# A transformer block with routed experts on one core: attention's DRAM exchange as one store and one load, and sequence 15 in it too

## The chip, the cores and the metric

One core of a Trainium2 chip runs the whole program. The metric is the device time of one execution in microseconds (us). Before the change it is 1090.54 us, the median of three runs (1088.64 to 1091.8).

## What is computed

Sixteen sequences of 256 tokens with 256 features pass through one block: a layer norm with a shift per sequence, attention with 16 heads of 64 features whose queries and keys are normalised per head, a residual, and then eight experts, each of which takes the 512 tokens of all 4096 with the highest gate. Everything is float32.

```python
h = _ln(x, ln1_g, ln1_b) + shift
qkv = (h @ Wqkv.T).reshape(b, n, 3, H, HD)
q = _ln(qkv[:, :, 0].transpose(0, 2, 1, 3), qn_g, qn_b)
k = _ln(qkv[:, :, 1].transpose(0, 2, 1, 3), kn_g, kn_b)
attn = softmax(einsum('bhnd,bhmd->bhnm', q, k) / sqrt(HD))
o = einsum('bhnm,bhmd->bhnd', attn, v)
x = x + o.transpose(0, 2, 1, 3).reshape(b, n, H * HD) @ Wout.T
gate = softmax(tok @ Wgate.T)
vals, idx = top_k(gate.T, bs // E)
y = gelu(ln(tok[idx]) @ fc1s.T + b1s) @ fc2s.T + b2s
tok = tok.at[idx].add(y * vals)
```

## The kernel before, in words

**Groups and quads.** For each sequence, `First` normalises and turns the tokens (`hT`). `Group(b, g, t)` multiplies 128 tokens by 512 columns of `wq`: g 0 and 1 are queries, 2 and 3 keys, 4 and 5 values. The mean over each head's 64 features is taken out of the weights beforehand (`center`, L600 to L607, once for each of 8 pieces), so that only the sum of squares is left to do: `square` on ACT, `stats` (L705) on DVE, `power` on POOL, `scale` (L721) on DVE. `Quad(b, d)` does four heads in two steps i of two heads j: `scores` (L813) on PE into four PSUM buffers `sc`, `maxima` (L821) on DVE, `exps` (L830) on ACT with the row sums, `invert` (L837), `normalise` (L841) on POOL, `product` (L900) on PE, `evict` (L915) on ACT. `Tail` projects, adds the residual, stores tokens and norms and computes the gates.

**Two ways to turn a tile.** Queries, keys and probabilities must change places between partitions and columns. Sequences 0 and 15 (`DIRECT`) do it on PE: `transposes` (L730, L881), then an ACT copy out of PSUM (L742, L888). The other fourteen use an exchange. DVE turns 32x32 blocks (L754, L851) into a tile `kb` or `pb`; `away` stores it (512 KB) to a DRAM tile whose rows hold four pieces of 1 KB and one of padding (L761, L859); `back` loads it with four DMAs of 128 KB, each to 32 partitions 32q to 32q+31 (L773, L873). Queries and keys then get gain and bias on ACT in `affine` (L781, L789). All these DMAs are issued by SP, in one queue.

**The order.** Every step is entered in a `Plan` with its engine, an assumed duration, what it needs and makes. `PLACES` holds one number for each step, found offline; the steps are issued in the order of these numbers, so each engine has a fixed order. Sorted by them, the first routing (`Routing.turn` L1028, then 30 rounds of `compare_less` L1091, `count_over` L1100 and `decide` L1115) follows the gates of sequence 14, with the later quads and the tail of sequence 15 between its rounds, and dummy matmuls (`fill`, L551) where PE has nothing else. The lists, the gather and the 16 expert jobs come after it.

The scores read the keys of an exchanged sequence piece by piece, so that their columns come in the order (k t m) in which `turn` cuts them:

```python
keys = plain(kTs[self.b]) if direct else (
    kTs[self.b].rearrange("p g k t h m -> p g h (k t) m")
)
```

Of the kernel before, what the change touches and what calls it, by code (L numbers as in the profile page):

```python
# [9 lines left out]
F32 = mybir.dt.float32  # L10
# [8 lines left out]
P = 128  # L19
# [15 lines left out]
SQ = 32  # L35
# [29 lines left out]
def kernel(  # L65
# [83 lines left out]
    def make_others():  # L149
# [21 lines left out]
    DIRECT = (0, B - 1)  # L171
# [11 lines left out]
        0.3, 0, 3.3, 4.02, 3.75, 5.04, 4.42, 7.26, 0, 0, 8, 9.39, 21.59, 15.62, 11.2, 13.11,  # L183
        17.01, 18.4, 0, 0, 0, 0, 0, 0, 0, 3.5, 4.21, 5.54, 4.52, 5.23, 6.09, 6.6, 7.26, 10.88,
        12.83, 15.02, 15.97, 19.79, 26.15, 26.82, 14.6, 16.55, 20.39, 21.18, 23.31, 28.69, 29.8,
        16.33, 18.28, 20.99, 23.06, 25.36, 27.79, 28.46, 20.58, 22.53, 23.91, 24.94, 27, 28.24,
        29.13, 24.1, 26.05, 33.83, 36.09, 29.35, 31.3, 32.01, 32.8, 34.94, 36.73, 37.55, 31.08,
        33.03, 33.74, 34.68, 36.66, 53.28, 54.22, 37.45, 40.14, 40.85, 42.51, 44.49, 48.92, 51.33,
        39.18, 41.13, 41.84, 44.39, 46.57, 52.83, 53.55, 47.04, 49.88, 49.37, 52, 32.81, 35.54,
        36.58, 38.73, 40.91, 41.63, 34.34, 35.13, 39.64, 41.35, 42.12, 38.46, 43.11, 35.71, 37.26,  # L190
        38.22, 40.69, 41.79, 42.61, 37.86, 39.18, 41.6, 42.67, 44.05, 40.42, 46.02, 47.26, 44.13,
        45.37, 46.16, 50.43, 53.73, 55.38, 45.97, 48.92, 51.34, 54.17, 54.89, 50.16, 57, 45.15,
        47.17, 47.96, 53.16, 63.68, 68.13, 47.77, 50.37, 52.25, 64.12, 67.64, 51.61, 70.34, 71.58,
        55.11, 56.95, 58.1, 60.54, 66.44, 67.15, 56.35, 57.14, 59.63, 78.31, 81.13, 59.36, 83.25,
        56.13, 59.53, 64.4, 68.49, 77.87, 78.83, 58.15, 59.06, 67.58, 80.48, 81.62, 66.42, 84.27,
        86.99, 74.97, 76.5, 77.37, 83.28, 91.94, 92.75, 77.1, 79.32, 82.37, 90.48, 91.2, 80.91,
        94.7, 81.36, 83.07, 83.86, 89.48, 96.74, 97.55, 85.48, 87.48, 90.39, 94.26, 96.51, 89.21,
        101.81, 103.78, 115.15, 119.13, 120.28, 120.28, 121.51, 122.02, 123.82, 124.54, 127.81,
        128.58, 118.62, 122.45, 124.6, 123.6, 124.46, 125.96, 131.29, 132, 134.85, 135.67, 0,
        14.5, 15.21, 24.51, 12.59, 13.3, 22.98, 42.23, 43.1, 51.1, 53.05, 53.76, 54.55, 57.55,  # L200
        58.75, 60.22, 62.17, 62.88, 63.82, 65.82, 66.61, 58.34, 60.44, 61.15, 61.94, 63.92, 65.21,
        66.01, 67.37, 70.57, 72.17, 76.37, 61.95, 63.9, 64.61, 65.7, 67.68, 68.47, 69.27, 70.63,
        73.83, 75.43, 80.28, 64.71, 66.66, 68.61, 70.56, 66.88, 68.83, 69.54, 70.33, 72.31, 73.1,
        71.36, 73.46, 74.17, 74.96, 77.7, 78.49, 73.24, 75.19, 75.9, 76.84, 79.1, 80.3, 81.1,
        82.46, 85.66, 87.26, 91.69, 75.99, 78.33, 79.7, 80.49, 82.47, 83.67, 84.47, 85.83, 89.03,
        90.63, 95.66, 78.75, 82.11, 85.14, 88.44, 82.38, 84.88, 86.03, 87.54, 88.6, 84.28, 85.07,
        88.45, 89.51, 87.27, 90.63, 92.63, 95.83, 97.43, 106.44, 90.92, 92.16, 93.24, 96.03,
        97.14, 92.76, 94.2, 96.94, 98.95, 95.76, 99.75, 101.11, 104.31, 105.91, 111.23, 114.89,
        95.72, 97.75, 98.54, 105.78, 106.84, 98.35, 104.27, 106.69, 108.65, 105.51, 109.45,
        111.11, 114.31, 116.23, 129.4, 100.79, 102.03, 102.82, 107.6, 111.66, 102.63, 105.23,  # L210
        108.51, 112.87, 106.47, 113.67, 115.03, 118.46, 120.66, 130.42, 131.51, 107.46, 109.86,
        111.01, 118.96, 120.13, 109.26, 110.05, 114.35, 118.52, 114.08, 125.1, 127.2, 130.51,
        133.3, 141.66, 108.48, 111.06, 112.93, 115.26, 116.69, 110.46, 111.97, 116.17, 117.3,
        114.85, 118.1, 119.46, 123, 125.2, 140.64, 142.75, 112.25, 115.02, 115.88, 121.61, 127.2,
        114.25, 117.33, 122.52, 129.35, 121.34, 130.15, 132.1, 135.7, 138.5, 144.42, 124.04,
        125.39, 126.18, 128.68, 131.68, 125.99, 127.14, 129.59, 132.81, 128.41, 133.61, 135.3,
        138.5, 140.5, 145.44, 148.04, 162.09, 166.05, 167.29, 167.2, 168.45, 170.6, 176.27,
        177.75, 178.81, 179.57, 165.56, 169.54, 171.6, 170.69, 171.55, 172.1, 179.26, 182.41,
        182.94, 184.62, 0, 25.96, 26.82, 28.77, 24.84, 27.58, 28.44, 80.92, 82.6, 87.02, 88.97,
        90.12, 91.3, 93.36, 94.15, 88.75, 90.7, 91.41, 93.18, 95.16, 96.53, 92.53, 95.16, 95.93,  # L220
        97.85, 99.83, 101.03, 101.83, 103.19, 106.39, 109.11, 113.89, 97.33, 99.5, 100.43, 101.22,
        103.23, 104.02, 105.91, 107.91, 111.11, 112.71, 118.29, 99.06, 106.19, 109.35, 116.84,
        102.83, 107.18, 108.05, 109.42, 112.27, 117.91, 104.71, 106.68, 107.45, 111.3, 113.48,
# [1414 lines left out]
```

## Time and profile before

| | before |
|---|---|
| median of three runs | 1090.54 us |
| the profiled execution | 1091.3 us |
| its span, first to last instruction | 1089.5 us |
| granted PE clock, mean | 0.993 |
| PE busy | 1050.4 us |
| POOL busy | 617.5 us |
| DMA: SP's and ACT's queue (q1), share of 16 engines | 69.9% |
| DMA packets under 2 KB | 139440 of 167700 |

PE is the tensor engine and PEld its weight loads, which overlap with matmuls; DVE, ACT and POOL are the vector, scalar and GpSimd engines, SP the one that issues DMAs. A row of a group names the line of the code, the engine, the operation, output and input tiles, shapes and the count, then busy time in all, the mean of one, and the idle time ahead of it with what ended it. Busy times are unions: two overlapping matmuls count once.

### The profile page before, as it was taken

To read this page: it belongs to the slowest core of one execution; us is meant where nothing else is said; L and a number is where in the kernel's file an instruction comes from. 1 tells how busy PE (TensorE), PEld (TensorE's weight loads), DVE (VectorE), ACT (ScalarE), POOL (GpSimd) and SP (SyncE) were. 2 spreads that over 40 slices of the span, in tenths; PEclk is the share of its full clock that TensorE was granted. 3 is DMA by queue.
4 is the path that set the end of the run, shared out by engine and by line. 5 is a ranking of instruction groups with operands and counts; after the bars stand their busy time and mean duration, and the time that the engine had idled before them with its cause. 6 is when DMAs were issued, how large, how long until landed. Compare 5 with 4: busy or idle time off the path is not lost. (4 is left out here: it accounts for less than half of the span.)

```text
span 1089.5 us, 18716 instructions
## 1 busy us (share of the span) xinstructions
PE 1050.4 (96%) x5611; PEld 686.6 (63%) x5611; DVE 809.4 (74%) x2257; ACT 592.3 (54%) x1656; POOL 617.5 (57%) x997
## 2 busy tenths in 40 slices
PE   6999999999999999999999999999988999999996
PEld 4555646555454655555565555656667888888885
DVE  6658888889788797898888887885678588655440
ACT  1768666666566665675666656675612322332331
POOL 3676776778667686667757666665501333333332
PEclk9999999999999999999999999999999999999998
DMA  6025899999999999998999999985130556655661
GB/s 214 1 78 165 269 276 304 291 281 257 283 292 280 280 299 290 289 280 263 277 299 286 265 302 265 321 260 164 61 102 20 149 161 199 186 171 163 192 203 20
DMA packets 167700, 238.56 MB, mean 219 GB/s; under 512 B 17328, under 2 KB 139440, under 8 KB 167600
## 3 DMA queue, kind: packets, MB, share of 16 engines
q1 hardware_dynamic: 159680, 227.08, 69.9%
q0 software_dynamic: 6144, 8.39, 4.2%
q10 hardware_dynamic: 1776, 1.90, 0.5%
q8 instruction: 45, 0.74, 0.3%
q14 instruction: 55, 0.45, 0.1%
HBM read 136.64 MB, written 100.66 MB: 218 GB/s over the span
## 5 line engine op out<-in xcount | busy, mean ns | idle before, releaser
L688 PE MATMUL pm<-wq,hT 128*128 128x512 f32 x768 | 362.1, 607 | 10.1 <-DVE qk L721 3.9
L841 POOL TENSOR_SCALAR pr<-pr,sums 128x256 f32<-128x256 f32 x512 | 237.6, 485 | 102.6 <-DVE sums L837 95.0
L830 ACT ACTIVATE pr<-sc,nmax 128x256 f32<-128x256 f32 x512 | 237.7, 482 | 92.3 <-DVE nmax L821 75.2
L688 PEld LDWEIGHTS pm<-wq,hT 128*128 128x128 f32 x768 | 137.1, 191 | 165.3 <-issue 131.3
L103 POOL TENSOR_TENSOR ss<-ss,neghalf 128x8 f32<-128x8 f32 x128 | 211.2, 1650 | 10.7
L821 DVE TENSOR_REDUCE nmax<-sc 128x2 f32<-128x512 f32 x256 | 165.3, 672 | 19.4 <-PE sc L813 19.1
L851 DVE STREAM_TRANSPOSE pb<-pr 128x512 f32<-128x512 f32 x224 | 150.0, 689 | 15.9 <-POOL pr L841 9.4
L813 PE MATMUL sc<-kT,qT 64*128 64x256 f32 x1024 | 136.8, 396 | 1.0 <-ACT kT L789 0.6
L701 ACT ACTIVATE sq<-pm 128x512 f32<-128x512 f32 x128 | 76.4, 605 | 102.5 <-PE pm L688 100.5
L900 PE MATMUL po<-prT,v 128*64 128x256 f32 x1024 | 129.0, 387 | 1.3 <-DMA prT<-blocks 1.3
L813 PEld LDWEIGHTS sc<-kT,qT 64*128 64x128 f32 x1024 | 91.3, 186 | 50.3 <-issue 28.9
L1319 POOL DMA_INDIRECT out<-y,idx x32 | 51.3, 1604 | 120.6 <-DVE y L1313 66.0
L1286 PE MATMUL ph<-xT,w 128*128 128x256 f32 x512 | 117.8, 383 | 0.0
L1302 PE MATMUL py<-w,hid 128*128 128x256 f32 x512 | 116.3, 380 | 0.0
L926 PE MATMUL pw<-wo,oT 128*128 128x256 f32 x512 | 115.3, 382 | 0.0
L926 PEld LDWEIGHTS pw<-wo,oT 128*128 128x128 f32 x512 | 96.2, 190 | 20.9 <-issue 6.0
L830 ACT ACTIVATION_READ_ACCUMULATOR pr<-sc,nmax 128x1 f32 x512 | 109.2, 213 | 0.0
L900 PEld LDWEIGHTS po<-prT,v 128*64 128x64 f32 x1024 | 66.5, 136 | 66.0 <-issue 20.1
L705 DVE TENSOR_REDUCE ss<-sq 128x8 f32<-128x512 f32 x128 | 85.0, 669 | 28.8 <-ACT sq L701 28.3
L1293 ACT ACTIVATE hid<-ph,vec 128x256 f32<-128x256 f32 x128 | 60.4, 474 | 84.4 <-PE ph L1286 79.4
L1302 PEld LDWEIGHTS py<-w,hid 128*128 128x128 f32 x512 | 95.6, 190 | 12.8
L1286 PEld LDWEIGHTS ph<-xT,w 128*128 128x128 f32 x512 | 95.4, 190 | 12.8
(141 smaller groups left out, 1098.3 us busy)
## 6 DMA issues: line engine op xcount, KB each, us to landing
blocks<-pb SPq DMA_DIRECT2D x112, 512.0 KB, 4.7
prT<-blocks SPq DMA_DIRECT2D x448, 128.0 KB, 4.1
kblocks<-kb SPq DMA_DIRECT2D x56, 512.0 KB, 4.1
w<-in_fc2T SPq DMA_DIRECT2D x16, 1024.0 KB, 5.8
w<-in_fc1T SPq DMA_DIRECT2D x16, 1024.0 KB, 8.3
qraw<-kblocks SPq DMA_DIRECT2D x112, 128.0 KB, 4.0
kT<-kblocks SPq DMA_DIRECT2D x112, 128.0 KB, 4.1
out<-tok SPq DMA_DIRECT2D x32, 128.0 KB, 3.9
```

The source lines that it names most:

```text
L103: nc.gpsimd.tensor_tensor(dst, src, neghalf[:, : src.shape[1]], ALU.pow)
L688: nc.tensor.matmul(self.pm, hTs[self.b][:, c, bass.ts(self.t, P)], wq[:, c, bass.ts(self.g, GW)], start=(c == 0), stop=(c == DC - 1),)
L705: nc.vector.tensor_reduce(self.ss[:, 0, :], self.sq.rearrange("p (h d) -> p h d", d=HD), AX.X, ALU.add,)
L813: nc.tensor.matmul(self.sc[i, j][:, t, :], qTs[self.b][rows, hp, bass.ts(t, P)], keys[rows, hp] if direct else keys[rows, hp // 4, hp % 4] ...
L821: nc.vector.tensor_reduce(self.nmax[i, j], self.sc[i, j], AX.X, ALU.max, negate=True)
L830: nc.scalar.activation(self.pr[i, j][:, t, :], self.sc[i, j][:, t, :], AF.Exp, bias=self.nmax[i, j][:, t : t + 1], scale=1.0, accum_out=se ...
L841: nc.gpsimd.tensor_scalar(self.pr[i, j][:, t, :], self.pr[i, j][:, t, :], self.sums[i][:, 1, j, t : t + 1], 1.0, ALU.mult, ALU.mult,)
L851: nc.vector.transpose(self.pb[i][:, :, :, j].rearrange("p k c t n -> p t k c n"), self.pr[i, j].rearrange("p t (k c m) -> p t k c m", c=TB ...
L900: nc.tensor.matmul(self.po[j * HD : (j + 1) * HD, i, :], vs[self.b][:, c, bass.ts(4 * self.d + 2 * i + j, HD)], prT[:, j, c] if self.b in ...
L926: nc.tensor.matmul(self.pw, oTs[self.b][:, hp // 2, self.t, hp % 2, :], wo[:, hp, :], start=(hp == 0), stop=(hp == HP - 1),)
L1286: nc.tensor.matmul(self.ph[f], self.w1[:, c, bass.ts(f, P)], self.xT[:, c, :], start=(c == 0), stop=(c == DC - 1),)
L1302: nc.tensor.matmul(self.py[i], self.hid[:, f, bass.ts(i, P)], self.w2[:, f, :], start=(f == 0), stop=(f == FC - 1),)
```

## The change

The exchange gets another map. A 128-wide piece goes to partitions 4m+q, q being one of four column pieces, instead of 32q+m. In DRAM the tile has no padding, and the partition order (m q) is then one run of it for each of the four blocks, so that `back` is one DMA of 512 KB to all 128 partitions. To make this the right order:

- the host puts the query and key columns of `Wqkv` in an order of (q, head, feature/4) within each group of 512, so `center`, `stats` and `scale` sum and scale over four pieces of 16 for each head; `center` takes three operations instead of two;
- for sequence 0, which still transposes its queries and keys on PE, `scale` writes them back in natural order, with a step of four words;
- the scores read the keys in natural token order (t k m), and `exps` of exchanged quads read PSUM with a step of four words, so that `pr` is written in the order (q c m).

Only sequence 0 is `DIRECT` now. `OFFS` are the quads that still turn their probabilities on PE: all four of sequence 0 and the quads 2 and 3 of sequence 15. Sequence 15's queries, keys and quads 0 and 1 (its first 8 heads) use the exchange. `PLACES` is new throughout: 3883 numbers for 3883 steps instead of 3863.

```diff
@@ -168,7 +168,7 @@
-    DIRECT = (0, B - 1)
+    DIRECT, OFFS = (0,), {(b, d) for b in (0, B - 1) for d in range(HP // 2)} - {(B - 1, 0), (B - 1, 1)}
...
@@ -180,349 +180,352 @@
     PLACES = (
...
@@ -599,12 +602,14 @@
         def center(g, c):
-            w3 = wq[:, c, bass.ts(g, GW)].rearrange("p (h d) -> p h d", d=HD)
+            w3 = wq[:, c, bass.ts(g, GW)].rearrange("p (q e d) -> p q e d", q=QB, e=8)
             ws = stat.tile([P, 8], F32, tag="ws", bufs=2, name="ws")
-            nc.vector.tensor_reduce(ws, w3, AX.X, ALU.add)
-            nc.vector.scalar_tensor_tensor(
-                w3, ws.unsqueeze(2).to_broadcast([P, 8, HD]), -1.0 / HD, w3, ALU.mult, ALU.add
-            )
+            nc.vector.tensor_reduce(ws, w3.rearrange("p q e d -> p e q d"), AX.XY, ALU.add)
+            nc.vector.tensor_scalar_mul(ws, ws, -1.0 / HD)
+            nc.vector.tensor_tensor(w3, w3, by_head(ws), ALU.add)
+
+        def by_head(x):
+            return x.unsqueeze(1).unsqueeze(3).to_broadcast([P, QB, 8, HD // QB])
         class Norm:
@@ -703,8 +708,8 @@
             def stats(self):
                 self.ss = stat.tile([P, 2, 8], F32, tag="ss", name="ss")
                 nc.vector.tensor_reduce(
-                    self.ss[:, 0, :], self.sq.rearrange("p (h d) -> p h d", d=HD),
-                    AX.X, ALU.add,
+                    self.ss[:, 0, :], self.sq.rearrange("p (q e d) -> p e q d", q=QB, e=8),
+                    AX.XY, ALU.add,
                 )
             def power(self):
@@ -718,10 +723,13 @@
                 if src is None:
                     self.qk = work.tile([P, GW], F32, tag="qk", bufs=3, name="qk")
                     engine, src = nc.vector, self.pm
+                if self.b in DIRECT:
+                    dst = self.qk.rearrange("p (e d q) -> p q e d", q=QB, e=8)
+                else:
+                    dst = self.qk.rearrange("p (q e d) -> p q e d", q=QB, e=8)
                 engine.tensor_tensor(
-                    self.qk.rearrange("p (h d) -> p h d", d=HD),
-                    src.rearrange("p (h d) -> p h d", d=HD),
-                    self.ss[:, 1, :].unsqueeze(2).to_broadcast([P, 8, HD]), ALU.mult,
+                    dst, src.rearrange("p (q e d) -> p q e d", q=QB, e=8),
+                    by_head(self.ss[:, 1, :]), ALU.mult,
                 )
             def transposes(self):
@@ -753,13 +761,13 @@
                     kb.append(work.tile([P, QB, TB, HP // 2, SQ], F32, tag="pb", bufs=3, name="kb"))
                 nc.vector.transpose(
                     kb[0][:, :, self.t],
-                    self.qk.rearrange("p (h q d) -> p q h d", q=QB, d=SQ),
+                    self.qk.rearrange("p (q h d) -> p q h d", q=QB, d=SQ),
                 )
             def away(self, kb):
-                self.blocks = dram.tile([QB, SQ, QB + 1, N], F32, tag="blocks", bufs=4, name="kblocks")
+                self.blocks = dram.tile([QB, SQ, QB, N], F32, tag="blocks", bufs=4, name="kblocks")
                 nc.sync.dma_start(
-                    self.blocks[:, :, :QB].rearrange("k d q n -> (k d) (q n)"),
+                    self.blocks.rearrange("k d q n -> (k d) (q n)"),
                     kb[0].rearrange("p q t h m -> p (q t h m)"),
                 )
@@ -769,10 +777,7 @@
                 else:
                     self.raw = self.keys()[:, self.g - 2]
                 raw = self.raw.rearrange("p k t h m -> p k (t h m)")
-                for q in range(QB):
-                    nc.sync.dma_start(
-                        raw[bass.ts(q, SQ)], self.blocks[:, :, q].rearrange("k d n -> d k n")
-                    )
+                nc.sync.dma_start(raw, self.blocks.rearrange("k d q n -> (d q) k n"))
             def affine(self):
                 if self.g < 2:
@@ -801,10 +806,11 @@
             def scores(self, i):
                 hp = 2 * self.d + i
-                direct = self.b in DIRECT
-                keys = plain(kTs[self.b]) if direct else (
-                    kTs[self.b].rearrange("p g k t h m -> p g h (k t) m")
-                )
+                whole = self.b in DIRECT
+                if whole:
+                    keys = plain(kTs[self.b])
+                else:
+                    keys = kTs[self.b].rearrange("p g k t h m -> p g h t k m")
                 for j in range(2):
                     self.sc[i, j] = ps.tile([P, TB, N], F32, tag="sc", bufs=4, name="sc")
                 for t in range(TB):
@@ -812,7 +818,7 @@
                         rows = slice(j * HD, (j + 1) * HD)
                         nc.tensor.matmul(
                             self.sc[i, j][:, t, :], qTs[self.b][rows, hp, bass.ts(t, P)],
-                            keys[rows, hp] if direct else keys[rows, hp // 4, hp % 4],
+                            keys[rows, hp] if whole else keys[rows, hp // 4, hp % 4],
                             start=True, stop=True,
                         )
@@ -827,8 +833,12 @@
                     self.sums[i] = stat.tile([P, 2, 2, TB], F32, tag="sums", name="sums")
                 self.pr[i, j] = work.tile([P, TB, N], F32, tag="pr", bufs=PRB, name="pr")
                 for t in range(TB):
+                    dst, src = self.pr[i, j][:, t, :], self.sc[i, j][:, t, :]
+                    if not ((self.b, self.d) in OFFS):
+                        dst = dst.rearrange("p (q c m) -> p q c m", q=QB, c=TB)
+                        src = src.rearrange("p (c m q) -> p q c m", q=QB, c=TB)
                     nc.scalar.activation(
-                        self.pr[i, j][:, t, :], self.sc[i, j][:, t, :], AF.Exp,
+                        dst, src, AF.Exp,
                         bias=self.nmax[i, j][:, t : t + 1], scale=1.0,
                         accum_out=self.sums[i][:, 0, j, t : t + 1],
                     )
@@ -855,9 +865,9 @@
             def away(self, i):
-                self.blocks[i] = dram.tile([QB, SQ, QB + 1, N], F32, tag="blocks", bufs=4, name="blocks")
+                self.blocks[i] = dram.tile([QB, SQ, QB, N], F32, tag="blocks", bufs=4, name="blocks")
                 nc.sync.dma_start(
-                    self.blocks[i][:, :, :QB].rearrange("k m q n -> (k m) (q n)"),
+                    self.blocks[i].rearrange("k m q n -> (k m) (q n)"),
                     self.pb[i].rearrange("p q c h t n -> p (q c h t n)"),
                 )
@@ -869,10 +879,7 @@
             def back(self, i):
                 prT = self.turned(i).rearrange("p (k n) -> p k n", k=QB)
-                for q in range(QB):
-                    nc.sync.dma_start(
-                        prT[bass.ts(q, SQ)], self.blocks[i][:, :, q].rearrange("k m n -> m k n")
-                    )
+                nc.sync.dma_start(prT, self.blocks[i].rearrange("k m q n -> (m q) k n"))
             def transposes(self, i, j):
                 self.pp[i, j] = ps.tile([P, TB, N], F32, tag="sc", bufs=4, name="pp")
@@ -891,7 +898,7 @@
                 if self.po is None:
                     self.po = ps.tile([P, 2, N], F32, tag="po", name="po")
-                if self.b in DIRECT:
+                if (self.b, self.d) in OFFS:
                     prT = self.prT[i].rearrange("p (h c n) -> p h c n", h=2, c=TB)
                 else:
                     prT = self.prT[i].rearrange("p (k c h n) -> p c h k n", k=QB, c=TB, h=2)
@@ -900,13 +907,13 @@
                         nc.tensor.matmul(
                             self.po[j * HD : (j + 1) * HD, i, :],
                             vs[self.b][:, c, bass.ts(4 * self.d + 2 * i + j, HD)],
-                            prT[:, j, c] if self.b in DIRECT else prT[:, c, j],
+                            prT[:, j, c] if (self.b, self.d) in OFFS else prT[:, c, j],
                             start=(c == 0), stop=(c == TB - 1),
                         )
...
             def evict(self):
                 oT = of_sequence(oTs, self.b, "oT", [P, HP // 2, TB, 2, P])[:, self.d]
-                if self.b in DIRECT:
+                if (self.b, self.d) in OFFS:
                     dst = oT.rearrange("p t i n -> p i t n")
                     src = self.po.rearrange("p i (t n) -> p i t n", t=TB)
                 else:
@@ -1412,13 +1419,13 @@
                         at(q + 1 + j, "DVE", 0.6, partial(a.maxima, i, j), [("sc",) + m], [nmax], [scs[j], nmax], lag=0.19)
                         at(q + 2 + j, "ACT", 0.96, partial(a.exps, i, j), [nmax], [sums], [scs[j], nmax, sums, pr], lag=0.28)
                         at(q + 5 + j, "POOL", 0.91, partial(a.normalise, i, j), [("inv",) + m], [pr], [pr, sums], lag=0.15)
-                        if b in DIRECT:
+                        if (b, d) in OFFS:
                             at(q + 6 + j, "PE", 0.44, partial(a.transposes, i, j), [pr], [pp], [pr, pp], lag=0.22)
                             at(q + 7 + j, "ACT", 0.49, partial(a.copy, i, j), [pp], [prT], [pp, prT], lag=0.21)
...
                             at(q + 6 + j, "DVE", 0.61, partial(a.turn, i, j), [pr], [pb], [pr, pb], lag=0.19)
                     at(q + 4, "DVE", 0.17, partial(a.invert, i), [sums], [("inv",) + m], [sums])
-                    if b not in DIRECT:
+                    if (b, d) not in OFFS:
                         at(q + 10, "SP", 0.36, partial(a.away, i), [pb], [(1, blocks)], [pb, blocks], lag=1.0)
                         at(q + 11, "DMA", 1.2, nothing, [(1, blocks)], [blocks], [pb], lag=2.0)
                         at(q + 14, "SP", 1.6, partial(a.back, i), [blocks], [(1, prT)], [blocks, prT], lag=0.0)
@@ -1602,6 +1609,7 @@
     def twice(v):
         return np.concatenate([v, v]).reshape(P, 1)
+    qk = a["Wqkv"][: 2 * H * HD].reshape(-1, 8, HD // 4, 4, D).transpose(0, 3, 1, 2, 4)
     vecs = np.concatenate(
         [
             columns(a["ln1_g"]), columns(a["ln1_b"]), columns(a["b_ada"]),
@@ -1615,7 +1623,7 @@
         "x": a["x"].reshape(NTOK, D),
         "condT": a["cond_1024"].T,
         "w_adaT": a["W_ada"].T,
-        "wqkvT": a["Wqkv"].T,
+        "wqkvT": np.concatenate([qk.reshape(-1, D), a["Wqkv"][2 * H * HD :]]).T,
         "woutT": a["Wout"].T,
         "wgateT": a["Wgate"].T,
...
```

## The prediction

> **What bounds the kernel now.** I read the page's first two parts, then the busy time by stage (the windows view), the groups of instructions with shapes kept apart, the timeline of PE around the routing, and the waits. The page first:
>
> ```profile
> span 1089.5 us, 18716 instructions
> ...
> PE 1050.4 (96%) x5611; PEld 686.6 (63%) x5611; DVE 809.4 (74%) x2257; ACT 592.3 (54%) x1656; POOL 617.5 (57%) x997
> ...
> DMA  6025899999999999998999999985130556655661
> ```
>
> PE works 1050.4 of 1089.5 us; 39 us is all that better cover could ever give, the rest must come from less PE work. The DMA digits are at 9 through the attention. By stage (columns: us, then busy us of PE, weight loads, DVE, ACT, POOL, each with its count, granted clock, DMA share, GB/s):
>
> ```profile
> 0.00:60.00 60.00, 49.21 (x208) 29.06 (x209) 35.49 (x76) 28.80 (x67) 32.23 (x61) 0.97 0.29 98
> 60.00:700.00 640.00, 630.80 (x3020) 355.85 (x3017) 536.66 (x1064) 416.18 (x1225) 444.12 (x760) 1.00 0.94 272
> 700.00:776.60 76.60, 76.51 (x449) 49.90 (x448) 48.94 (x106) 50.74 (x153) 43.03 (x81) 1.00 0.69 207
> 776.60:819.30 42.70, 35.55 (x250) 25.52 (x249) 31.28 (x170) 14.05 (x40) 12.50 (x26) 1.00 0.20 66
> 837.50:1060.00 222.50, 222.14 (x1454) 194.71 (x1451) 138.30 (x759) 73.61 (x151) 76.01 (x63) 1.00 0.59 175
> ```
>
> From 60 to 776.6 us PE is the bound (707.3 of 716.6), and again in the experts. Between them lies the first routing: a serial chain of 30 rounds, compare on DVE (L1091), count on PE (L1100), decide on DVE (L1115). It cannot begin before sequence 14 has left its gates and PE has turned them (L1028):
>
> ```profile
> 776.64 0.40 PE L1028 MATMUL pgT<-ident,gate_of 128*128 128x128 f32 x2
> 778.85 0.18 PE L1100 MATMUL pc<-cnt,twice 128*128 128x1 bf16 x1
> ...
> 793.67 0.18 PE L1100 MATMUL pc<-cnt,twice 128*128 128x1 bf16 x1
> ...
> 794.68 0.16 PE L1100 MATMUL pc<-cnt,twice 128*128 128x1 bf16 x1 [0.34 <-DVE reach L1091]
> ...
> 819.28 0.16 PE L1100 MATMUL pc<-cnt,twice 128*128 128x1 bf16 x1 [0.34 <-DVE reach L1091]
> ```
>
> A round alone takes 1.0 us (late in the chain, only fills lie between). The first 11 counts span 14.8 us for 10 gaps, because sequence 15 still shares PE and DVE. So the end time is: PE work ahead of the turn, plus the chain, plus fixed work. PE work moved out of the chain's stretch gives nothing by itself; PE work removed ahead of the turn counts in full.
>
> **The change part by part.** The rows used (count, then busy us, then mean ns):
>
> ```profile
> L830 ACT ACTIVATE pr<-sc,nmax 128x256 f32<-128x256 f32 x512 | 237.7, 482 | 92.3 <-DVE nmax L821 75.2 <-POOL pr L841 7.8 <-POOL ss L103 4.8
> L881 PE MATMUL pp<-ident,pr 128*128 128x128 f32 x128 | 18.9, 278 | 1.6 <-POOL pr L841 1.2
> L730 PE MATMUL pq<-ident,qk 128*128 128x128 f32 x64 | 9.0, 277 | 1.8 <-DVE qk L721 1.8
> L998 DVE TENSOR_TENSOR gate_of<-gates,smax 128x224 f32<-128x224 f32 x1 | 0.8, 765 | 0.0
> L990 DVE TENSOR_TENSOR gates<-gates,smax 128x224 f32<-128x224 f32 x1 | 0.4, 391 | 0.0
> ```
>
> *Sequence 15 exchanges.* Its 32 query and key transposes (half of L730's 64: 4.5 us) and 32 of L881's 128 (4.7 us) go: **-9.2 us** of PE, and in the old order all of them stand ahead of the turn, where PE is 99.9% busy. In the new order two more steps stand ahead of it, the two scores of quad (15,3), 8 matmuls each at a pitch of 134 ns (L813: 136.8 us for 1024): **+2.1 us**. The other PE steps ahead of the turn are the same set in both orders.
>
> What replaces the transposes runs elsewhere: 16 DVE turns (L754 695 ns, L851 689 ns: 11 us), 8 exchanges, 4 affine steps (L781 820 ns, L789 1246 ns). ACT loses 16 evictions and copies. DVE has 27.7 us free between 700 and 776.6 us; the turns and four maxima brought forward (672 ns) take 13.7 of it, so it would be some 90% busy where 640 us of attention run at 84%: cost 0 to +3 us, taken as 0. SP gets 16 issues there; behind them wait the norm and token stores of sequences 13 and 14 and the first expert's weights, used 60 us later.
>
> *The chain.* Two scores and their maxima, exps and inverts leave it. Of its 40.4 us for 29 gaps, 11.4 are above 29 lone rounds: 4.8 in the first ten gaps, the rest where the projections and gates of sequence 15 stand, which stay. So bounds 0 and -4.8; a score and its two maxima fill 2.4 us of the two longest early gaps (1.07 on PE, then 1.29 on DVE), each 1.2 us above a lone round: taken **-2.5 us**.
>
> *The exchange itself.* One load of 512 KB replaces four of 128 KB (L773, L873). SP saves three issues of 0.43 us in each of 168 exchanges, and the landing four issues later (1.3 us). It is hidden: PE waited for prT 1.3 us and its weight loads 3.1 us in the whole run, and I find the products starting a median of 6.0 us after their data had landed (landing against L900 in the timeline). Gain 0 to 4 us; the row it is nearest to is that wait of 1.3 us on the last few products, and I take 0. On the other side, the store's row padding of 1 KB goes and all lengths become powers of two. With a DMA share of 0.94 to 1.02 a load slower by more than some 5% would be PE's bound; no row here shows an unpadded exchange. The nearest transfer, xs (256 KB in 1 KB pieces to 128 partitions), lands in 4.6 us beside 4.1 for a 128 KB quarter, so twice the bytes cost 0.5 us more. I take 0.
>
> [...]
>
> *Exps read PSUM with a step of four words.* 464 of 512 exps (all but six quads). No row shows a strided read on ACT. Below: a DVE write with a step of two words (L1172, 424 ns for 256) costs what its plain neighbour does (L1184, 405 ns). Above: L998 against L990, same operation and size, the first writing with a step of 128 bytes: (765 - 391)/224 = 1.67 ns an element, so +427 ns an exp, 198 us of ACT. Sixteen bytes is nearer to eight than to 128: I take 0 and keep both ends.
>
> [...]
>
> *Start.* Centring gets a small extra multiply, 8 times 0.15 us (a 128x8 DVE copy, L969, takes 156 ns); DVE has no gaps between 15 and 27 us, so **+1.2**. Sequence 0's eight scales now write with that same step of four words: 0 to +0.86 us each (1.67 times 512), four of them ahead of the first query and key transposes: 0 to +3.4, taken **+1.0** (a guess within the bounds). The new order puts both first query groups ahead of the keys and PE's value group earlier; the start's PE gaps are 10.8 us in 60, so 0 to -2.4, taken **-1.2**. Sum **+1.0**.
>
> *Elsewhere* the reduction and the scale run over 16-word pieces instead of 64, and the scores read keys in three dimensions. The product's two forms show no price for pieces: contiguous and 64-word runs have one pitch in the timeline (109 and 106 ns). L754 reads in 32-word pieces at 695 ns, L851 plain at 689. Zero.
>
> **Sum:** -9.2 + 2.1 - 2.5 + 1.0 = -8.6 us. The profiled execution took 1091.3 us around its span of 1089.5; it stands 0.8 above the median 1090.54. So 1082.7 for such an execution, **1081.9** for the median.
>
> **Rivals.** *Half the gain is late again.* The exchange of sequence 15 is a longer path than its transposes (store and load, 4.7 + 4.1 us landing, with SP and DVE on the way). If the quads (15,0) and (15,1) reach their products late, or the start pays its upper bound, 3 to 5 us return: 1086 to 1088. For it: a DVE nine tenths full. Against it: their products lie behind both projections of sequence 14 (7.2 us of PE) that need nothing of 15.
>
> *ACT becomes the bound (slower).* Place: L830 in 60 to 760 us. If a four-word step costs one more element time, by ACT's own slope (1246 - 820)/512 = 0.83 ns, an exp costs +213 ns, ACT +95 us in the attention: 80% of it. A step of two exps then ends 0.43 us later, a pair 0.85; in the timeline a dozen of 126 scores begin less than that after the exps that free their PSUM, and the copies of po and v behind them on ACT shift as much. I price that at 12 us: 1094. At +427 ns ACT would need 416 + 190 of 640 us, with the in-order waits for nmax (75 us) between: some 35 us, 1117. It decides from about +150 ns an exp. Against it: ACT has 35% free.
>
> *DMA becomes the bound.* A tenth more time per byte at a share of 0.97 would stretch 640 us by some 45: 1127. *The change does only what it says of the queue:* if transposes stayed in number, nothing but hidden time would move: 1090; the diff's conditions speak against it.
>
> **How the numbers follow.** Forecast 0.57 (1078 to 1087 by its own bounds), half gain 0.16, ACT 0.19, DMA 0.05, nothing 0.03. This kernel's measurement tells some 0.3% (3.3 us) from no change: faster means below 1087.3, slower above 1093.8. Faster 0.57 + half of 0.16 = 0.65; same 0.08 + 0.03 + 0.03 of ACT = 0.14; slower 0.21. The range runs from the forecast's lower bound, 1077, into the ACT case, 1099; beyond lie some 0.12 above and 0.05 below.
>
> **What would show it.** L730 x32 and L881 x96; the turn (L1028) some 6 us earlier; the chain near 37.9 us from first count to last; L830's mean still near 482 ns; PE above 98% in the attention; L721's form in sequence 0 longer. Wrong, if L830 rises beyond 630 ns with PE waiting on ACT, or if products wait for prT.

## The result

The kernel after takes **1074.89 us** (median of 4 runs, 1072.86 to 1077.49), the kernel before 1090.61 beside it: ratio 0.9859, 95% interval [0.9833, 0.9885]. It is 15.7 us faster; 8.6 were forecast. The profiled execution took 1075.44 us, at a mean granted PE clock of 0.986. Its page:

```profile
span 1073.7 us, 17767 instructions
...
PE 1039.4 (97%) x5547; PEld 681.8 (64%) x5547; DVE 822.4 (77%) x2281; ACT 588.9 (55%) x1646; POOL 617.5 (58%) x997
...
DMA  6014889888987898888888898889430656665661
```

PE is busy 11.0 us less (1050.4 to 1039.4), and the span is 15.8 us shorter: idle time went as well. The DMA digits fell from 9 to 8. By stage, kernel after (columns as before: us, then busy us of PE, weight loads, DVE, ACT, POOL, clock, DMA share, GB/s):

```profile
60.00:700.00 640.00, 639.62 (x3102) 365.81 (x3100) 548.41 (x1087) 430.16 (x1259) 456.78 (x783) 1.00 0.82 279
700.00:760.20 60.20, 58.82 (x332) 36.52 (x330) 50.70 (x109) 38.80 (x127) 37.53 (x71) 1.00 0.93 315
760.20:763.70 3.50, 2.42 (x21) 1.74 (x19) 1.04 (x5) 3.13 (x10) 3.21 (x6) 1.00 0.88 270
763.70:803.40 39.70, 31.59 (x216) 24.17 (x216) 26.76 (x156) 7.68 (x15) 6.64 (x16) 0.91 0.20 70
820.70:1043.20 222.50, 222.13 (x1456) 194.71 (x1453) 139.23 (x762) 73.29 (x152) 75.83 (x63) 1.00 0.60 174
```

From 60 to 700 us PE was idle for 9.2 us before (640.00 - 630.80) and is for 0.4 us now; the DMA share fell from 0.94 to 0.82 although more bytes a second move (272 to 279 GB/s). The turn comes at 760.18 instead of 776.64 us, **16.5 us earlier**; 6.1 were forecast. Then 1.3 us are lost to the first count, 0.8 gained in the chain (39.7 instead of 40.4 us), and from the first expert on nothing differs (253.0 against 253.2 us to the end).

The timeline of PE around the turn, kernel after (start, duration, engine, line, operation, in brackets the idle time before it):

```profile
759.17 1.08 PE L907 MATMUL po<-prT,v 128*64 128x256 f32 x8 [0.98 <-DMA prT<-blocks]
760.18 0.50 PE L1035 MATMUL pgT<-ident,gate_of 128*128 128x128 f32 x2
...
762.64 1.08 PE L907 MATMUL po<-prT,v 128*64 128x256 f32 x8 [1.08 <-DMA prT<-blocks]
763.66 0.18 PE L1107 MATMUL pc<-cnt,twice 128*128 128x1 bf16 x1
```

Two products of sequence 15 wait for their exchange, on either side of the turn, and a third waits 0.80 us behind the first count. And the groups that the prediction named (count, busy us, mean ns; the second is for sequence 0 alone):

```profile
L840 ACT ACTIVATE pr<-sc,nmax 128x256 f32<-128x256 f32 x512 | 237.8, 480 | 101.5 <-DVE nmax L827 77.6 <-POOL ss L103 9.1 <-DVE sums L847 5.7
...
L730 DVE TENSOR_TENSOR qk<-pm,ss 128x512 f32<-128x512 f32 x8 | 8.6, 1074 | 6.7 <-POOL ss L103 5.8 <-PE pq L738 0.8
L738 PE MATMUL pq<-ident,qk 128*128 128x128 f32 x32 | 4.5, 278 | 1.6 <-DVE qk L730 1.4 <-ACT v L702 0.2
...
L888 PE MATMUL pp<-ident,pr 128*128 128x128 f32 x96 | 14.2, 287 | 0.0
```

The transposes went as counted, and the exps with their step of four words in PSUM cost what they did (480 against 482 ns). Sequence 0's scales, which write with that step in SBUF, rose from 679 to 1074 ns; the other 120 scales of the kernel after, without the step, take 677.

### The profile page after: what moved, and what is told of

Same layout as the page of the kernel before. It is cut to its first block, busy times and chain, and to the rows that moved or that the text cites. A ratio compares the mean times of both kernels' runs of the same rounds, so it can differ in the third digit from the quotient of the medians.

```text
span 1073.7 us, 17767 instructions
## 1 busy us (share of the span) xinstructions
PE 1039.4 (97%) x5547; PEld 681.8 (64%) x5547; DVE 822.4 (77%) x2281; ACT 588.9 (55%) x1646; POOL 617.5 (58%) x997
## 5 line engine op out<-in xcount | busy, mean ns | idle before, releaser
L861 DVE STREAM_TRANSPOSE pb<-pr 128x512 f32<-128x512 f32 x232 | 154.2, 687 | 7.4 <-POOL pr L851 6.9
L730 DVE TENSOR_TENSOR qk<-pm,ss 128x512 f32<-128x512 f32 x128 | 89.7, 702 | 22.8 <-POOL ss L103 20.8
```

Of the source, the lines that this page charges most:

```text
L730: engine.tensor_tensor(dst, src.rearrange("p (q e d) -> p q e d", q=QB, e=8), by_head(self.ss[:, 1, :]), ALU.mult,)
L861: nc.vector.transpose(self.pb[i][:, :, :, j].rearrange("p k c t n -> p t k c n"), self.pr[i, j].rearrange("p t (k c m) -> p t k c m", c=TB ...
```

## The experiments

**Theory E:** the exchange itself was no hidden transfer; its new form gives most of the gain. **Rival O:** the new order and sequence 15's missing transposes give it. Within E: is it SP's queue (fewer issues, theories N and Q) or the transfers (S, spread: the partitions that a load covers; T: fewer and larger loads)?

The runs on the load and the queue at a glance; those on the order, the turn and the pitch follow in the text. Ratios are to the kernel before on the same chip; PE idle is 640 us less PE's busy time from 60 to 700 us; shares are from 200 to 700 us, that of SP being the time of its issues; packet means are of all packets of 1 KB from 100 to 700 us, the issue is the median of the loads of probabilities (`prT`). All from the traces.

| kernel | ratio [95%] | PE idle us | DMA share | SP share | 1 KB packet ns | load issue ns |
|---|---|---|---|---|---|---|
| before | 1 | 9.2 | 0.99 | 0.64 | 66.3 | 430 |
| after | 0.9859 [0.9833, 0.9885] | 0.4 | 0.86 | 0.28 | 52.2 | 371 |
| e1 exchange alone | 0.9900 [0.9886, 0.9915] | 0.6 | 0.86 | 0.27 | 52.2 | 374 |
| e5 before, no padding | 1.0077 [1.0063, 1.0091] | 13.0 | 0.98 | 0.63 | 67.8 | 430 |
| e10 four loads of 32 neighbours | 1.0012 [0.9999, 1.0026] | 9.9 | 0.99 | 0.63 | 66.4 | 430 |
| e11 two loads of 64 neighbours | 1.0040 [1.0021, 1.0058] | 12.0 | 0.99 | 0.50 | 69.0 | 608 |
| e6 four loads of every 4th | 1.0407 [1.0382, 1.0433] | 32.2 | 0.80 | 0.81 | 54.6 | 603 |
| e9 one load, 3 tiny issues | 0.9950 [0.9931, 0.9968] | 3.2 | 0.86 | 0.54 | 51.9 | 387 |
| e12 one load, more traffic | 1.0023 [1.0007, 1.0039] | 8.2 | 0.93 | 0.30 | 51.6 | 371 |
| e13 control of e12 | 0.9890 [0.9867, 0.9913] | 0.3 | 0.86 | 0.28 | 52.1 | 374 |
| e14 tiny issues and traffic | 1.0561 [1.0524, 1.0598] | 47.5 | 0.86 | 0.50 | 52.5 | 387 |

**Which part of the change.** Four kernels divide it.

```diff
e1: kernel after, but
-    DIRECT, OFFS = (0,), {... all quads of 0 and 15 ...} - {(B - 1, 0), (B - 1, 1)}
+    DIRECT, OFFS = (0, B - 1), {... all quads of 0 and 15 ...}
     and the PLACES of before
e2: kernel before (old exchange), but DIRECT, OFFS and PLACES of after
e3: kernel after with e1's DIRECT and OFFS; its PLACES fitted to the extra steps
e4: kernel before with e3's PLACES
```

> The new exchange (map 4m+q, no padding, one load) in the old order, with sequence 15 back on PE as before. Theory E: the 10 us beyond the forecast come from the shorter exchange, which lets PE run without stalls in the attention; then some 8 to 10 us faster than before less 2 us that the start pays: 1082 to 1084 us, PE idle between 60 and 700 us about 1 instead of 9 us. Theory O: they come from the new order, the exchange being hidden; then 1091 to 1093 us, idle still about 9 us.

> The old exchange (32q+m, padded rows, four loads) with the new order and sequence 15 in the exchange as in the changed kernel. Theory E: loses the 10 us: about 1083 us, PE idle in the attention about 9 us. Theory O: keeps them and saves the 2 us that the start pays: 1073 us.

> The changed kernel with sequence 15's transposes back on PE (16 steps of four transposes and their 16 copies out of PSUM, put in the new order near the turns that they replace). If sequence 15's part is worth its 64 transposes: 9 us slower than the changed kernel, 1084 us; up to 4 us more where my placing holds PE up. If its worth was the earlier start of the routing only by other means: within 3 us of 1075.

> The new order alone: old exchange, sequence 15 on PE in the places of the run before it. Theory E: as before the change or slower, 1090 to 1095 us. Theory O: 1081 to 1085 us, as the kernel with the new exchange in the same order, or 2 us faster.

Measured: 0.9900; 1.0065 [1.0048, 1.0081]; 0.9890 [0.9875, 0.9906]; 1.0081 [1.0057, 1.0105]. On that chip (before 1093.06 us) the exchange alone gives 11 us. Sequence 15 in it is worth some 3.5 more by these ratios, which are from two chips (0.9890 to 0.9859), and 5.4 by the profiled spans (e3 1079.1, after 1073.7 us). The order by itself does nothing clear beside the new exchange (0.9900 to 0.9890) and costs 9 us beside the old one; that it was made for a shorter exchange is the likely reason, not a shown one. E holds, O falls. The attention of e1, by the windows view, is that of the kernel after:

```profile
60.00:700.00 640.00, 639.39 (x3091) 363.85 (x3089) 545.77 (x1082) 426.68 (x1257) 450.00 (x774) 1.00 0.82 278
```

How the old exchange reached PE shows one step behind PE's own waits. PE's three longest, and ScalarE's and VectorE's for DMAs, from 60 to 760 us in the kernel before, and then ScalarE's in the kernel after (us in total, times, longest):

```profile
PE pm L688 <- ACT v L697: 1.9, 2, 1.2
PE pg L952 <- ACT hT L659: 1.3, 1, 1.3
PE po L900 <- DMA prT<-blocks: 1.3, 1, 1.3
...
ACT kT L789 <- DMA kT<-kblocks: 12.3, 13, 1.9
ACT qT L781 <- DMA qraw<-kblocks: 8.9, 8, 3.0
...
DVE st L615 <- DMA xs<-in_x: 7.5, 5, 3.3
DVE pb L851 <- DMA kblocks<-kb: 5.0, 6, 2.0
```

```profile
ACT kT L794 <- DMA kT<-kblocks: 2.4, 3, 1.2
```

ACT's affine steps stood for 21.2 us waiting for landed queries and keys, and what follows them on ACT in its order, evictions of `v`, `hT`, `tokT` and `oT` among it, can come late by that. Those are the names on which most of PE's short waits are booked in the kernel before (`v` 1.9 and 0.5 us, `hT` 1.3 and 0.8, `tokT` 0.8, `oT` 0.6); the kernel after has two rows of 0.4 us and one for prT of 1.0. DVE waited for DMAs as well: 16.5 us before, for input tiles and for stores that had to free `kb` and `pb`, and 1.7 after. That these waits are what reached PE is read from the rows, not tested one by one. The exchange itself got shorter by a little: the store of `pb` lands a median of 4.1 us after its issue in e1 instead of 4.7, and the one load 5.2 us after its issue, where the last of four quarters landed 5.7 us after the first was issued.

**Which property of the load.** One edit each, on the kernel before (e5) and on e1 (e6, e10, e11, e9):

```diff
e5   dram.tile([QB, SQ, QB + 1, N], ...)  ->  dram.tile([QB, SQ, QB, N], ...)
e6   for q in range(QB): dma_start(prT[q::QB], blocks[:, :, q] as "m k n")
e10  for h in range(4): dma_start(prT[32h : 32h + 32], blocks[:, 8h : 8h + 8] as "(m q) k n")
e11  for h in range(2): dma_start(prT[64h : 64h + 64], blocks[:, 16h : 16h + 16] as "(m q) k n")
e9   one load, then 3 x dma_start(junk[n : n + 1, :], ident[:1, :])
```

> The kernel before with one edit: the rows of the exchange's buffer in DRAM are no longer padded by 1 KB; four loads, the old map of partitions and the old order stay. The exchange alone was worth some 11 us (e1_exchange_alone), and its parts are one load for four, the partitions 4m+q for 32q+m, and no padding. Theory N (one load: three issues on SP and three completions fewer): nothing changes, ratio 1.00. [...] If the padding cost something (rows 1 KB apart from alignment), this shows it: below 0.995. If the power-of-two pitch hurts, above 1.005 and longer packets than 66 ns in 1 KB pieces.

> e1_exchange_alone (new exchange with sequence 15 on PE, order of before) with one edit: each exchange is again loaded by four loads of 128 KB, but each of them to the 32 partitions 4m+q, four apart, not to 32 neighbours. Theory N (number of loads): SP issues 168 times 3 more, the gain of e1 goes: ratio 1.00, DMA share in the attention back near 0.94, 1 KB packets near 66 ns. Theory S (spread): ratio 0.99 as e1, packets near 52 ns although SP issues four times. In between, 0.993 to 0.997, both have a part.

> e1_exchange_alone with each exchange loaded by four loads of 32 neighbouring partitions, in the new map 4m+q (so each of them reads pieces of 1 KB that lie four to a row of 4 KB). Issue count and partitions of a load as in the kernel before; DRAM side as in the new exchange. Theory Q: four issues, 430 ns each as before, ratio 1.00. That 603 ns in four_spread_loads came from the step of four partitions would be shown by 430 here. Theory T says the same ratio if packets are back at 66 ns; if they are at 52 ns, it says 0.99.

> e1_exchange_alone with each exchange loaded by two loads of 64 neighbouring partitions. Theory Q: one issue more than e1 for each exchange, SP issues some 0.37 to 0.40 of the time and is still idle most of it, so the loss is far from proportional: 0.990 to 0.993. Theory T: between e1 and before by the number of loads, 0.993 to 0.997.

> e1_exchange_alone (new exchange, sequence 15 on PE, order of before) with one addition: behind each of the 168 loads SP issues three stores of 512 bytes from one partition, to rows of DRAM that nobody reads. They move 0.26 MB in all, so they add nothing to the DMA's load; they cost SP its issuing time, 3 x 0.33 to 0.43 us an exchange. Theory Q (SP's queue: four_spread_loads lost 44 us with a DMA share of only 0.80, while each issue took 603 ns and SP issued 0.81 of the time from 200 to 700 us; the kernel before issues 0.64 of it with 60 to 130 ns between issues; the exchange's gain is that the queue becomes short): most of e1's gain is lost again, ratio 0.996 to 1.00, PE idle in 60 to 700 us up from 0.6 to 5 or more us. Theory T (transfer: fewer, larger loads land sooner and the DMA engines are relieved, 0.99 to 0.86): ratio 0.99 as e1, PE idle under 1.5 us.

Measured: e5 1.0077: the old exchange needed its padding (packets 67.8 ns, PE idle 13.0 us). e6 1.0407, a miss by 55 us for S, whose packets it confirms: they are short, and yet the kernel is far slower. e10 1.0012. e11 1.0040, worse than any theory had it. e9 0.9950: about half of the gain is gone with the exchange's transfers unchanged.

Packets first. Loads to 32 neighbours take 66.3 and 66.4 ns a packet, to 64 neighbours 69.0, to 32 partitions four apart 54.6, to all 128 52.2. e6 and e10 have loads of one size and number, so it is the partitions that a load covers, not its size; nor is it how full the engines are, for e12 has 51.6 ns at a share of 0.93. Loads to 64 neighbours are no better than to 32 (e11 beside e10). Why the partitions matter no run tells.

Then the queue. SP in the timeline, kernel before and then e1, over the same twelve microseconds (start, time for the merged issues):

```profile
400.11 2.03 SPq L773 DMA_DIRECT2D kT<-kblocks  x4
402.24 2.26 SPq L873 DMA_DIRECT2D prT<-blocks  x4
404.73 0.34 SPq L859 DMA_DIRECT2D blocks<-pb  x1
405.35 2.10 SPq L873 DMA_DIRECT2D prT<-blocks  x4
407.54 0.38 SPq L761 DMA_DIRECT2D kblocks<-kb  x1
```

```profile
399.73 0.33 SPq L866 DMA_DIRECT2D blocks<-pb  x1
400.18 0.36 SPq L879 DMA_DIRECT2D prT<-blocks  x1
401.40 0.33 SPq L766 DMA_DIRECT2D kblocks<-kb  x1
```

In these microseconds SP before goes from one issue to the next, and each store stands behind a group of loads; in e1 it waits for work. Over 60 to 760 us SP waits 293 us before and 582 in e1.

There is a second price of an issue. In the traces SP's DMAs signal one of eight semaphores in turn (966 of 971 steps from one issue to the next in the kernel before), and 829 of its 972 issues wait for the one that they signal themselves, so for the landing of the DMA eight issues earlier. With four loads to an exchange SP waited 18 us between 60 and 760 us for loads to land (e10: 17; e6, with its long issues: none), with one load not at all (after, e1). In e9 it waited 90 us for them: its tiny stores take most of the eight. So e9's 5.5 us are not issuing time alone. No run separates this price from the time of the issues, and in both e9 differs from the old exchange, whose issues take longer (430 ns a load, 252 a tiny store) and wait less.

In e6 every issue is longer (603 ns for a load, 525 to 535 for the unchanged stores against 332), and SP issues 0.81 of the time: its queue is the likely bound. The windows view of e6:

```profile
60.00:700.00 640.00, 607.78 (x2869) 342.01 (x2868) 505.49 (x1004) 396.39 (x1163) 418.54 (x721) 0.98 0.77 256
```

PE is idle for 32 us at the lowest DMA share of the table: the share says nothing of a queue that issues too slowly. Why issues got longer there and in e11 no run tells.

But e11 needs SP for less time than e9 (0.50 against 0.54), its SP waits 1.6 us for loads to land against 90, and it loses everything, e9 only half. So the transfers have a part of their own.

**Queue and transfers apart.** On e1; e12 has 26 stores of 1 MB from ScalarE's queue (two in each of sequences 1 to 13), e13 the same 26 issues of 512 bytes, e14 both e12's stores and e9's tiny issues:

```diff
e12  + nc.scalar.dma_start(more[2 * self.b + self.g - 2], wq[:, 0, :2048])
e13  + nc.scalar.dma_start(more[2 * self.b + self.g - 2, :1, :128], wq[:1, 0, :128])
```

> e1_exchange_alone with 26 added stores of 1 MB (two in each of sequences 1 to 13, ahead of the key affine steps) of a resident weight tile to rows of DRAM that nobody reads, issued from ScalarE's queue, not SP's. By 174 ns for a packet of 4 KB they add some 72 us of 16 engines' time to 640: DMA share 0.82 to some 0.93, as in the kernel before, with SP's issues as in e1. Theory T (the DMA engines' load): PE idle in 60 to 700 us from 0.6 to 4 us or more, ratio 0.994 to 1.00. Theory Q (SP's queue alone): 0.99 as e1.

> The control of e12: the same 26 issues on ScalarE's queue, each of 512 bytes. Ratio 0.99 as e1 if ScalarE's issuing costs nothing; what it loses to e1 is to be taken from what e12 loses.

> The three tiny issues on SP for each exchange (as in e9_three_tiny_issues) and the added traffic of e12 together. If the two causes add up: the loss of e9 (5.5 us) plus the loss of e12, ratio near 1.00, the kernel before. If the queue and the load are one line that waits (each matters more with the other): above 1.00.

Measured: e12 1.0023, e13 0.9890, e14 1.0561. With SP's queue as short as in e1 the added traffic alone costs 14.8 us (1094.71 less 1079.93) and PE is idle again (windows view of e12):

```profile
60.00:700.00 640.00, 631.82 (x3023) 357.21 (x3024) 536.61 (x1063) 416.06 (x1226) 445.11 (x760) 1.00 0.90 315
```

This is almost the row of the kernel before. So neither theory is enough alone: more load on the DMA engines costs time with SP's queue as short as in e1 (T, by e12), and more issues cost time with the exchange's transfers unchanged, by issuing or by the waits that they bring (Q, by e9). How the 11 us of the old exchange divide between the two is not shown.

The two don't add in e14: e9's 5.5 us and e12's 14.8 would make 1100, e14 takes 1153.83. But its trace shows a wait of its own. SP's longest waits for the added stores, from 60 to 760 us:

```profile
SPq L888 <- DMA more<-wq: 54.2, 13, 7.5
SPq L873 <- DMA more<-wq: 30.4, 7, 7.5
```

L888 are the tiny stores, L873 the stores of `pb`. In all SP stood 95 us for landings of the added stores of 1 MB, in e12 not at all: with the tiny issues in the queue, the eight semaphores come round fast enough to make SP wait for them. So e14 does not show that the two causes of the old exchange make each other worse; it may be this link that does it.

**The waits at the turn.** e7 is the kernel after with other places for seven steps, e8 the kernel after itself, on the same chip:

```diff
e7  Routing.turn ahead of the second product of quad (15,0); that product and those of (15,1)
    behind the counts 29, 28 and 26; first product of (15,2) behind count 24
```

> The kernel after with other places for seven steps: the routing's turn stands ahead of the second product of quad (15,0), and the products of quads (15,0) and (15,1), which waited for prT 0.98, 1.08 and 0.80 us between the turn and the third count, stand behind the first counts. Theory W (these waits are on the path to the end): gate_of is ready at 757.9, so the turn begins near 758.2 instead of 760.18 and the first count near 760.3 instead of 763.66; some of it is lost where a product delays a count, so 2 to 3 us faster than the kernel after: ratio to before near 0.984. The other view (the chain's later stretch is bound by sequence 15's projections and gates, so an earlier start only lengthens it): same time as the kernel after.

> The kernel after, unchanged, so that the others of this call stand beside it on one chip: ratio 0.986 to before.

Measured: 0.9855 [0.9838, 0.9872] and 0.9848 [0.9834, 0.9863]: the same. e7's turn came at 757.40 instead of 758.69 us, its first count at 759.84 instead of 762.38, but its chain took 45.4 us instead of 39.4. The postponed products, and all that ACT and DVE do behind them, still have to pass between the rounds, and the rounds ran at a lower clock: the mean granted clock over the chain is 0.81 in e7 and 0.91 in e8. In e7 it was 0.50 from 762.2 to 772.4 and from 775.8 to 782.6 us, in e8 only for one stretch of 6.8 us. So W's gain did not come with this order; what the waits for prT would be worth at a full clock is not shown.

**The pitch.** The blocks of an exchange 132 KiB apart, in the kernel after (e15) and in e12 (e16):

```diff
-  dram.tile([QB, SQ, QB, N], ...);      store to blocks as "(k d) (q n)"
+  dram.tile([QB, SQ + 1, QB, N], ...);  store to blocks[:, :SQ] as "k d (q n)"
```

> The kernel after with one edit: the four blocks of an exchange lie 132 KiB apart in DRAM instead of 128 KiB (4 KB of padding between blocks; one store and one load as before). If the power-of-two pitch costs the new exchange something, 1 KB packets get shorter than 52.2 ns; since PE is already busy 639.6 of 640 us of the attention, the time can fall by no more than some 1 us there and 2 us at sequence 15's waits for prT: ratio 0.983 to 0.986. If the pitch doesn't matter: 0.9855, packets 52 ns.

> e12_more_traffic (new exchange, sequence 15 on PE, order of before, 26 MB of added stores) with blocks 132 KiB apart. There the DMA engines set the time, so a pitch that matters shows: packets shorter than 51.6 ns and a ratio clearly under 1.0023, by 3 us or more. If it doesn't matter: 1.00.

Measured: 1.5127 [1.5097, 1.5158] and 1.5486 [1.5449, 1.5522], misses of more than 570 us, and no answer to the question: with the gap the store can no longer be written as one run of 128 rows, its outermost dimension is now 4. Windows view of e15:

```profile
60.00:700.00 640.00, 443.90 (x1747) 236.78 (x1746) 309.45 (x611) 248.28 (x726) 261.88 (x453) 0.83 0.45 150
```

DMA is busy 0.45 of the time, and from 60 to 760 us SP waits 268 us for stores of `pb` to land. SP's queue has 5632 packets of 4 bytes instead of the 7744 of the kernel after, which are 16 for each of its 484 issues: 2112 fewer, 12 for each of 176 stores. If each engine that works on a store writes one of these packets, a store ran on 4 engines here, not 16; this is an estimate from the counts, no view shows the engine of a packet, and no run has the gap without this form of the store. Whether the power-of-two pitch costs the new exchange anything stays open.

## Why the prediction was wrong

**The exchange: 0 taken, 10.1 us measured** (spans of before and e1, 1089.5 and 1079.4). e1 has the cost of the start in it as well (its first projection begins at 121.05 us instead of 119.35), so the exchange itself gave rather more. This is the step that failed: "It is hidden: PE waited for prT 1.3 us [...] Gain 0 to 4 us; the row it is nearest to is that wait [...] and I take 0." The row only counts waits that end at a landing. PE's 9.2 idle us were spread over nine rows, eight with names of ACT and DVE; the DMA rows of these two engines, 21.2 and 16.5 us, were the next step back and weren't read. The products' slack of 6.0 us was a median, too, and of the probabilities' exchange only; of the 84 affine steps of queries and keys 21 waited for their load. And the prediction saw the DMA share of 0.97 as a danger from a slower load, not as the reason why a faster one would help. Its remark that twice the bytes cost 0.5 us more was no ground for a load to all 128 partitions either: e1 beside e10 and e11 shows that the partitions make the difference. The lower end of the forecast, 1078 in one place and 1077 in another, is also not what its terms add up to: -9.2, +2.1, -4.8 for the chain, -1.2 for the start and -4 for the exchange make 1073.4 us. Even those 4 us were less than half of what the exchange gave.

**Sequence 15 and the order: -8.3 us of turn taken (-9.2 + 2.1 - 1.2), -6.0 measured** (e1's turn 766.17, after 760.18). By parts: sequence 15 moves the turn by 7.5 us (e3 767.70 to 760.18) where 9.2 were taken; PE's 1.4 idle us from 700 us to the turn, the wait for prT among them, make most of the difference. Of the 7.5 the whole time keeps 5.4; the rest is lost at the first count and in the chain. The order alone adds 1.5 (e1 to e3), where 0.9 was taken.

**From turn to first count: nothing taken, +1.3 measured**, the product that waited 1.08 us for prT. It is the rival "half the gain is late again" in small; moving that product, in e7, won nothing.

**The chain: -2.5 taken, -0.8 measured.** The first ten gaps fell from 14.8 to 11.5 us, 3.3 less, somewhat more than taken. But gaps 11 to 14 took 6.6 us instead of four lone rounds of 1.0. The windows view of the kernel after shows a lower clock there:

```profile
763.70:775.20 11.50, 6.47 (x53) 3.93 (x53) 8.37 (x51) 5.18 (x10) 5.15 (x12) 0.93 0.02 7
775.20:781.80 6.60, 6.60 (x38) 4.79 (x37) 3.33 (x20) 1.17 (x2) 0.00 (x0) 0.60 0.00 0
```

PE was busy 6.5 of 11.5 us, and the next 6.6 us had a mean clock of 0.60; in finer windows it is 1.00 up to 773.6 us and 0.50 from there to 780.4. Four transposes took 1.06 us there instead of 0.64. In e3, which has the same order and its clock back at 1.00 earlier, the third and fourth of these rounds took 1.11 and 1.13 us; at that pace the four would take some 4.5, so by this estimate some 2.1 of the 2.6 us are the clock's. In the kernel before PE was busy 12.7 of the 14.8 us of its first gaps and kept a clock of 1.00, and e1 is the same; in e3 PE was busy 6.8 of 11.1 us, and 3.4 us at 0.50 followed. So the thinner work is the likely cause of the lower clock; no run tests it alone.

**The start: +1.0 taken, about right.** The strided scales cost 0.40 us each (0 to 0.86 given), the extra multiplies 0.17 (0.15 taken). Sequence 0's first projection begins 0.9 us later than before (120.28 against 119.35 us) and in e8, the same kernel, 0.3 earlier: the size of this term is no larger than what two executions differ by. The scale's DVE write to SBUF with a step of four words does pay (1074 against 679 ns). **The exps: 0 taken, 0 measured:** ScalarE's read of PSUM with that step cost nothing (480 against 482 ns). **Sequence 15's exchange on DVE: 0 taken;** DVE was busy 50.7 of 60.2 us before the turn, and PE's waits for it come to 0.4 us.

**The rivals.** ACT's bound fell with the 480 ns. "DMA becomes the bound" had the right resource and the wrong sign: the new load took fewer nanoseconds a byte, 52.2 a KB instead of 66.3. What the missing padding costs, e5 shows for the old exchange, 0.8%; for the new one no run tells.

## What to carry to other kernels

When an engine is 98% busy and its few idle microseconds are booked on many names, ask what those engines waited for, before calling a transfer hidden. A DMA share of 0.99 and a queue with few pauses between issues stood here beside an exchange whose speed-up gave 11 us. Try one load to all 128 partitions, and look at the store's outermost dimension too: here packets of 1 KB took 52.2 ns with one such load and 66.4 to 69.0 with loads to 32 or 64 neighbours (e10, e11), three issues more for each exchange cost 5.5 us (e9), and the kernel whose stores have an outermost dimension of 4 instead of 128, for blocks 132 KiB apart, took 1.51 times as long as the one before (e15). An order that costs nothing beside one exchange can lose beside another (9 us here). And a run that adds work to a queue can add waits too: read the queue's own waits before adding up its cost.

## What the hardware showed that was not expected

- The time of an issue on SP depends on the load: 371 ns (128 partitions), 430 (32 neighbours), 608 (64 neighbours), 603 (32 partitions four apart); in the last case the unchanged stores rose from 332 to between 525 and 535 ns as well.
- With the blocks 132 KiB apart, and so with stores whose outermost dimension is 4 instead of 128 (e15), the kernel took 1.51 times as long as the one before (ratio 1.5127), and a store left 12 packets of 4 bytes fewer.
- The granted clock was 0.50 for 6.8 us, from 773.6 us in the kernel after, behind 13.4 us in which PE was busy for 8.6; none of its pauses there was longer than 1.1 us.
- SP's DMAs take turns on eight semaphores (966 of 971 steps in the kernel before), and 829 of 972 issues wait for their own. SP waited 18 us for loads to land with four of them to an exchange (before), not at all with one (after).
- Three stores of 512 bytes for each exchange, 0.26 MB in all, cost 5.5 us (0.9900 to 0.9950), and 59 us beside the added traffic (1153.83 less 1094.71); SP then waited 90 us for loads to land in the first case, and 95 us for the added stores in the second.
